# First output projection ahead of the older batch's second one, group norm among the latter's products, first attention begun on half of q and k

## The chip, the cores and the metric

One core of one Trainium2 chip runs the whole program in one launch. The metric is the device time in microseconds; the kernel before takes 4062.5 us (median of 3 runs, 4062.24 to 4063.74). Engines are named as in the profile: PE is TensorE, with its weight loads as PEld, DVE is VectorE, ACT is ScalarE, POOL is GpSimd, and SP is the queue of SyncE, from which nearly all transfers are issued.

## The reference, cut to what matters

Eight batches of 1024 tokens with 512 channels, all float32. Each passes two layers, and each layer is a group norm, an attention and an output projection that is added to the layer's input:

```python
# layer 0: 16 heads of 32 channels
x = x + proj(attention(_gn(x) @ w_qkv, heads=16), w_proj, b_proj)
# layer 1: 4 heads of 128 channels, with position logits
x = x + attention(_gn(x) @ Wq, _gn(x) @ Wk, _gn(x) @ Wv, heads=4, pos_emb_w, pos_emb_h) @ Wo
```

The group norm takes the mean and the variance over all tokens of 16 neighbouring channels, so it cannot begin before the whole x of its batch is there, and no product of the layer can begin before the norm has ended. No batch depends on another.

## The kernel before, in words

Everything is kept transposed, channels on partitions: an activation of one batch is a "block" of 128 x 4 x 1024 floats (2 MB), and eight blocks fit on chip (`BLOCKS`, taken in turn by the tag "block"). What does not fit is put away in DRAM and fetched again (`put_away`, `fetch`, L209 and L216).

**Projections.** Each of the eight weight matrices is applied in seven products instead of eight (a Strassen-like form). `forms` (L319 to L322) makes the sums of the input's quarters on DVE, partly in place. A projection is two units, u = 0 and u = 1, and `seven` makes one unit: seven products into three PSUM banks x, y, z. Between its products stand small operations: y is read by DVE into `a` (L359) after its first product and into `b` (L367) after its second, and only then may the next product accumulate into y. `Plain` puts a result into a block, `Onto` adds it to the fetched x (L418 on POOL, L423 and L425 on DVE). Unit u gives channel chunks u and u + 2. `Stream` holds the order in which weight tiles are loaded (`plan`), one unit ahead; `project_T` and `project_rows` run two units each.

**First attention** (`attention_0`): 64 steps for each batch, over four channel chunks m, two halves h of the queries and eight key blocks j. A step is a score product `ps` (L516, one buffer of four banks), an exponential on ACT (L524), a product with v into `acc` (L535) and a running sum `es` of the exponentials on DVE (L544 for the first two, L546 after that). Eight steps end with the product `sums` (L556), a normalisation on DVE and POOL (L482 to L504), which writes over q.

**Second attention** (`attention_1`): 64 steps of full 128-row products, run as one stretch, with the loading and the norm of the coming batch woven in.

**The order around the change.** The loop over b runs 9 times. Iteration b runs the first attention of batch b (here) beside a list `rest`, in this order: `after_1` of batch b-2 (past: projection WO, result written out), `after_0` of batch b-1 (last: projection WP), `norm_1` of b-1, `second` of b-1 (q, k, v and position logits of the second attention), `attention_1` of b-1 with the load of b+1 (coming), `before_0` of b+1 (q, k, v of the first attention). Parts are Python generators that yield what they cost, two for each product. `side_by_side` emits one step of the attention whenever its share of the total cost is due. `ALONE` is cost that is charged with no product behind it: while norm_1 runs, only attention steps are emitted. A scheduler then orders instructions by readiness, so that the built order differs somewhat from the emitted one. `woven(main, side, start, gap)` puts one piece of a side part behind every gap-th piece of the main part.

**The start.** Batch 0 is loaded and normed, then all six units of q, k and v run with nothing beside them, then iteration 0 runs the first attention of batch 0 beside the load and `before_0` of batch 1.

Of the kernel before, what the change touches and what calls it, by code (L numbers as in the profile page):

```python
# [27 lines left out]
def quick_path(  # L28
# [131 lines left out]
    class Stream:  # L160


        def __init__(self, plan):
            self.plan = [(m, rows, u) for m, rows in plan for u in range(2)]
            self.tiles = {}
            self.at = -1
            for i in ORDER:
                self.load(0, i)
# [77 lines left out]
    def group_norm(st, xT, name):  # L246

        mv = st.pop("mv")

        def averages(out, src, tag):  # L250
            total = small.tile([P, 2], F32, tag=f"total{tag}", name=f"total{tag}_{name}")
            nc.vector.tensor_reduce(
                total, src.rearrange("p (g k) -> p g k", k=GROUP_CHANNELS), axis=AX.X, op=ALU.add
            )
            nc.vector.tensor_scalar(
                out.rearrange("p (g k) -> p g k", k=GROUP_CHANNELS),
                total.unsqueeze(2).to_broadcast([P, 2, GROUP_CHANNELS]),
                1.0 / GROUP_CHANNELS,
                None,
                op0=ALU.mult,  # L260
            )

        turned = small.tile([P, 32], F32, tag="turned", name=f"turned_{name}")
        nc.vector.transpose(turned, mv)
        avg = small.tile([P, 2, 32], F32, tag="avg", name=f"avg_{name}")
        averages(avg[:, 0, :], turned, 0)

        nc.vector.tensor_sub(turned, turned, avg[:, 0, :])
        nc.vector.tensor_mul(turned, turned, turned)
        averages(avg[:, 1, :], turned, 1)  # L270
        back = small.tile([P, 2, 32], F32, tag="back", name=f"back_{name}")
        nc.vector.transpose(back.rearrange("p a c -> p (a c)"), avg.rearrange("p a c -> p (a c)"))
        mean = back[:, 0, :CC]
        var = small.tile([P, CC], F32, tag="var", name=f"var_{name}")
        nc.vector.scalar_tensor_tensor(
            var, back[:, 0, CC : 2 * CC], GN_EPS, back[:, 1, :CC], op0=ALU.add, op1=ALU.add
        )
        rstd = small.tile([P, CC], F32, tag="rstd", name=f"rstd_{name}")
        nc.gpsimd.tensor_tensor(rstd, var, neg_half, op=ALU.pow)
        yield 0  # L280
        for cc in range(CC):
            nc.vector.tensor_scalar(
                xT[cc],
                xT[cc],
                mean[:, cc : cc + 1],
                rstd[:, cc : cc + 1],
                op0=ALU.subtract,
                op1=ALU.mult,
            )
        yield 0  # L290


    in_place = [False]
# [156 lines left out]

        return [[x[n * HC + u][:, h * NB : (h + 1) * NB] for h in range(NH)] for n in range(2)]

    def project_T(fs, m, y, name):

        for u in range(2):
            stream.unit(m, False, u)
            yield from seven(fs, u, False, Plain(halves(y, u)), f"{name}_{u}")

# [46 lines left out]

    def attention_0(q, k, v, b):

        steps = [(m, h, j) for m in range(CC) for h in range(NH) for j in range(NT)]
        state = {}

        def front(m, h, j):
            name = f"0_{b}_{m}_{h}_{j}"
            ps = psum.tile([P, HB, NB], F32, tag="ps", name=f"ps_{name}", bufs=1)
            for r in range(HB):
                rows = slice(r * D0, (r + 1) * D0)
                nc.tensor.matmul(  # L516
                    ps[:, r, :],
                    k[m][rows, j * P : (j + 1) * P],
                    q[m][rows, h * NB : (h + 1) * NB],
                    start=True,  # L520
                    stop=True,
                )
            e = mem.tile([P, HB, NB], F32, tag="e0", name=f"e_{name}", bufs=2)
            nc.scalar.activation(e, ps, AF.Exp, scale=D0 ** -0.5)  # L524
            return e

        def back(m, h, j, e):
            name = f"0_{b}_{m}_{h}_{j}"
            if j == 0:
                state["acc"] = psum.tile([P, NB], F32, tag="acc", name=f"acc_{name}", bufs=1)  # L530
                state["first"] = e
            acc = state["acc"]
            for r in range(HB):
                c0 = (m * HB + r) * D0
                nc.tensor.matmul(  # L535
                    acc[r * D0 : (r + 1) * D0, :],
                    v[:, j, c0 : c0 + D0],
                    e[:, r, :],
                    start=(j == 0),
                    stop=(j == NT - 1),  # L540
                )
            if j == 1:
                state["esum"] = mem.tile([P, HB, NB], F32, tag="es0", name=f"es_{name}", bufs=1)
                nc.vector.tensor_add(state["esum"], state["first"], e)  # L544
            elif j > 1:
                nc.vector.tensor_add(state["esum"], state["esum"], e)  # L546
            if j < NT - 1:
                return
            nc.scalar.copy(q[m][:, h * NB : (h + 1) * NB], acc)
            state["ended"] = (m, h, state["esum"])  # L550

        def finish(m, h, esum):
            name = f"0_{b}_{m}_{h}"
            su = psum.tile([P, NB], F32, tag="acc", name=f"sums_{name}", bufs=1)
            for r in range(HB):
                nc.tensor.matmul(  # L556
                    su[r * D0 : (r + 1) * D0, :],
                    ones[:, :D0],
                    esum[:, r, :],
                    start=True,  # L560
                    stop=True,
                )
            normalise(q[m][:, h * NB : (h + 1) * NB], su, name)

        pending = None
        for at in steps:
            if "ended" in state:
                finish(*state.pop("ended"))
            e = front(*at)
            if pending is not None:  # L570
                back(*pending)
            pending = (*at, e)
            yield 2
        back(*pending)
        yield 1
        finish(*state.pop("ended"))
# [98 lines left out]
    def load(b, st):  # L675
# [19 lines left out]
        st["xn"] = forms(x, f"xn0_{b}")  # L695
        yield 0

    def before_0(b, st, hook=None):

        fs = st.pop("xn")  # L700
# [110 lines left out]
    PRODUCT = 2 * len(ORDER) * HC  # L811
    SECOND = 3 * PRODUCT - 8

    ALONE = 5

    WQ0, WK0, WV0 = [Matrix(w_qkv, i * C, f"qkv{i}") for i in range(3)]
    WP, WQ1, WK1 = Matrix(w_proj, 0, "p"), Matrix(Wq, 0, "q1"), Matrix(Wk, 0, "k1")
    WV1, WO = Matrix(Wv, 0, "v1"), Matrix(Wo, 0, "o")
    FIRST = [(WQ0, False), (WK0, False), (WV0, True)]
    plan = list(FIRST)  # L820
    for b in range(B + 1):
        if b == B:
            plan.append((WP, False))
        if b >= 2:
            plan.append((WO, False))
        if 1 <= b < B:
            plan.append((WP, False))
        if b >= 1:
            plan += [(WQ1, False), (WK1, False), (WV1, True)]
        if b + 1 < B:  # L830
            plan += FIRST
    plan.append((WO, False))

    states = [{} for _ in range(B)]
    WQ0.add_up(nc.vector, nc.scalar, nc.gpsimd, keep=True)
    run(load(0, states[0]))
    for m in (WK0, WV0):
        m.add_up(nc.vector, nc.sync, nc.gpsimd, keep=True)
    stream = Stream(plan)

# [2 lines left out]
            m.add_up(nc.gpsimd, nc.gpsimd, nc.gpsimd)  # L843
            yield 0

    run(before_0(0, states[0]))
    for b in range(B + 1):
        rest, total = [], 0
        s = [None] * 2 + states + [None] * 2
        past, last, here, coming = s[b : b + 4]  # L850
        incoming = load(b + 1, coming) if coming is not None else iter(())

        def forms_0(b=b, st=last):
            st["ao0"] = forms(st["q0"], f"ao0_{b - 1}")

        def forms_past(b=b, st=past):
            forms_1(b - 2, st)

        def forms_last(b=b, st=last):
            forms_1(b - 1, st)  # L860

        if last is not None:
            norm = norm_1(b - 1, last)
            if here is None:
                rest.append(after_0(b - 1, last, forms_past))
                rest.append(woven(later(after_1, b - 2, past), norm, 1, 4))
            else:
                if past is not None:
                    rest.append(after_1(b - 2, past, forms_0))
                    total += PRODUCT  # L870
                rest.append(later(after_0, b - 1, last))
                rest.append(chain([ALONE], (cost + ALONE for cost in norm), marked()))
                total += PRODUCT + 3 * ALONE
            rest.append(later(second, b - 1, last))
            rest.append(woven(later(lambda st: attention_1(*st.pop("at")), last), incoming, 4, 6))
            total += SECOND
        else:
            rest.append(incoming)
        if coming is not None:
            before = later(before_0, b + 1, coming, forms_last if last is not None else None)  # L880
            rest.append(before if last is not None else woven(before, other_sums(), 2, 7))
            total += 3 * PRODUCT
        if here is not None:
            side_by_side(attention_0(here["q"], here["k"], here["v"], b), chain(*rest), total)
        else:
# [494 lines left out]
```

## Time and profile before

| what | value |
|---|---|
| time | 4062.5 us |
| profiled span | 4059.8 us |
| PE busy | 3848.8 us, 95% |
| DVE busy | 2531.9 us, 62% |
| ACT busy | 1719.5 us, 42% |
| POOL busy | 601.6 us, 15% |
| one iteration from b = 2 to b = 6 | about 491 us (the product x_wo begins one at 1341.7 and the next at 1832.6) |
| bytes moved | 234.18 MB, mean 58 GB/s |

The page shows one profiled execution. Its first part gives the busy time of each engine, its second part the span in 40 slices. A busy PE is not PE at its peak, since matmuls are pipelined; what can be won without fewer products is the time in which PE has nothing to do, 211 us here. Answers of the trace name an instruction by engine, line, operation and tiles. In a timeline the columns are start, duration, instruction, count of records, and in brackets the idle time of the engine just before it with what ended that. A product of `seven` is 16 records (x16) or 32 (x32) for v.

### The profile page before, as it was taken

The numbers are of one execution on the slowest core, as the hardware profiler recorded it, in microseconds if no ns is written. First come the engines' busy times: TensorE is split into PE (matmuls) and PEld (weight loads), VectorE is DVE, ScalarE is ACT, GpSimd is POOL, SyncE is SP. The second block draws the span as 40 slices with busy tenths as digits, with TensorE's granted clock in tenths as the row PEclk, the third lists the DMA queues.
The fourth block names the chain that finished last, engine by engine and source line by source line (L and its number), as shares of the span: only waits on it lengthen the run. The fifth ranks groups of instructions, "written<-read, shape, count | busy, mean of one in ns | idle before, by whom it ended". The sixth has DMA issues, their size and how long they took to land.

```text
span 4059.8 us, 71621 instructions
## 1 busy us (share of the span) xinstructions
PE 3848.8 (95%) x30338; PEld 1417.6 (35%) x30338; DVE 2531.9 (62%) x2915; ACT 1719.5 (42%) x1761; POOL 601.6 (15%) x396
## 2 busy tenths in 40 slices
PE   6898899998999989999999999999999998999998
PEld 3232244232443324432244323433234332244353
DVE  5776665576655867458564685646856568664544
ACT  1454443444434444344443444444444444543132
POOL 1331111121111211112110111101111111111101
PEclk9999999999999999999999999999999999999999
DMA  5320120141201512014120231203311031110401
GB/s 143 118 86 26 48 59 6 37 122 50 59 6 38 129 49 58 7 47 131 37 53 12 88 85 36 53 19 95 79 37 45 26 98 54 33 63 8 115 29 22
DMA packets 498694, 234.18 MB, mean 58 GB/s; under 512 B 286368, under 2 KB 478144, under 8 KB 497344
## 3 DMA queue, kind: packets, MB, share of 16 engines
q1 hardware_dynamic: 495232, 214.79, 19.8%
q0 software_dynamic: 2608, 13.70, 0.9%
q8 instruction: 241, 3.95, 0.4%
q10 hardware_dynamic: 528, 1.05, 0.1%
q14 instruction: 85, 0.70, 0.1%
HBM read 170.72 MB, written 58.72 MB: 57 GB/s over the span
## 4 chain that ended last, share of the span: by engine, by line
PE 86%; DVE 7%; ACT 5%; issue 1%; DMA 1%; POOL 0%; SPq 0%; DVEq 0%; ACTq 0%; POOLq 0%
PE ps L516 12%; PE ps L626 11%; PE acc L638 11%; PE acc L535 11%; PE y_q L299 4%; PE y_k L299 3%; PE y_v L299 3%; PE ps L627 3%; ACT e L524 3%; PE x_v L299 3%; PE x_k L299 3%; PE x_q L299 3%; PE z_q L299 3%; PE z_v L299 2%; PE z_k L299 2%; PE y_wp L299 2%
## 5 line engine op out<-in xcount | busy, mean ns | idle before, releaser
L524 ACT ACTIVATE e<-ps 128x2048 f32<-128x2048 f32 x512 | 961.6, 1878 | 873.4 <-PE ps L516 749.1
L546 DVE TENSOR_TENSOR es<-es,e 128x2048 f32<-128x2048 f32 x384 | 899.3, 2342 | 504.5 <-ACT e L524 503.0
L516 PE MATMUL ps<-q,k 32*128 32x512 f32 x4096 | 613.1, 654 | 127.5 <-ACT e L524 127.3
L535 PE MATMUL acc<-e,v 128*32 128x512 f32 x4096 | 557.5, 617 | 12.9 <-ACT su L482 11.9
L629 ACT ACTIVATE e<-ps 128x512 f32<-128x512 f32 x512 | 305.7, 597 | 581.4 <-PE ps L627 551.2
L626 PE MATMUL ps<-q,k 128*128 128x512 f32 x1024 | 523.7, 593 | 0.0
L638 PE MATMUL acc<-e,v 128*128 128x512 f32 x1024 | 521.9, 592 | 0.0
L649 DVE TENSOR_TENSOR es<-es,e 128x512 f32<-128x512 f32 x384 | 287.0, 747 | 267.3 <-ACT e L629 266.5
L627 PE MATMUL ps<-posT,sel 128*128 128x512 f32 x512 | 406.7, 794 | 0.0
L504 POOL TENSOR_TENSOR q<-q,su 128x512 f32<-128x512 f32 x128 | 199.2, 1557 | 1381.7 <-DVE su L500 1339.3
L516 PEld LDWEIGHTS ps<-q,k 32*128 32x128 f32 x4096 | 166.6, 186 | 533.4 <-ACT e L524 267.2
L626 PEld LDWEIGHTS ps<-q,k 128*128 128x128 f32 x1024 | 193.6, 190 | 246.2 <-issue 239.4
L638 PEld LDWEIGHTS acc<-e,v 128*128 128x128 f32 x1024 | 193.1, 189 | 146.7 <-issue 105.2
L535 PEld LDWEIGHTS acc<-e,v 128*32 128x32 f32 x4096 | 82.0, 109 | 409.3 <-issue 352.1
L612 DVE TENSOR_TENSOR posT<-pp,posT 32x512 fp32r<-32x512 f32 x128 | 111.2, 869 | 157.8 <-ACT posT L611 157.3
L544 DVE TENSOR_TENSOR es<-e,e 128x2048 f32<-128x2048 f32 x64 | 173.1, 2704 | 35.7 <-ACT e L524 35.7
L484 DVE STREAM_TRANSPOSE tu<-su 128x512 f32<-128x512 f32 x128 | 90.7, 709 | 116.3 <-ACT su L482 116.0
L611 ACT CAST posT<-pp 32x512 fp32r<-32x512 f32 x128 | 104.8, 819 | 132.2 <-DVE posT L612 87.4
L482 ACT COPY su<-sums 128x512 f32<-128x512 f32 x128 | 74.9, 585 | 160.2 <-PE sums L556 92.1
L408 POOL TENSOR_TENSOR v<-b_v,p_v 128x512 f32<-128x512 f32 x32 | 67.3, 2104 | 499.8 <-ACT p_v L373 479.3
L408 POOL TENSOR_TENSOR k<-b_k,p_k 128x512 f32<-128x512 f32 x32 | 64.0, 1999 | 513.7 <-ACT p_k L373 513.7
L627 PEld LDWEIGHTS ps<-posT,sel 128*128 128x128 f32 x512 | 97.3, 190 | 122.5 <-issue 122.5
(188 smaller groups left out, 4404.1 us busy)
## 6 DMA issues: line engine op xcount, KB each, us to landing
w_qkv<-ws_qkv SPq DMA_DIRECT2D x168, 128.0 KB, 2.5
xs<-in_x SPq DMA_DIRECT2D x256, 64.0 KB, 2.6
d<-x0T SPq DMA_DIRECT2D x32, 512.0 KB, 3.0
x1T<-d SPq DMA_DIRECT2D x32, 512.0 KB, 6.4
d<-x1T SPq DMA_DIRECT2D x32, 512.0 KB, 3.6
x2T<-d SPq DMA_DIRECT2D x32, 512.0 KB, 6.0
out<-ot SPq DMA_DIRECT2D x256, 64.0 KB, 2.0
w_qkv<-in_L_conv_w_qkv SPq DMA_DIRECT2D x126, 128.0 KB, 2.2
```

Of the source, the lines that this page charges most:

```text
L299: ins = nc.tensor.matmul(out[columns, :], weights[:, columns], moving, start=start, stop=stop, skip_group_check=open_sum,)
L504: nc.gpsimd.tensor_tensor(dst, dst, su, op=ALU.mult)
L516: nc.tensor.matmul(ps[:, r, :], k[m][rows, j * P : (j + 1) * P], q[m][rows, h * NB : (h + 1) * NB], start=True, stop=True,)
L524: nc.scalar.activation(e, ps, AF.Exp, scale=D0 ** -0.5)
L535: nc.tensor.matmul(acc[r * D0 : (r + 1) * D0, :], v[:, j, c0 : c0 + D0], e[:, r, :], start=(j == 0), stop=(j == NT - 1),)
L544: nc.vector.tensor_add(state["esum"], state["first"], e)
L546: nc.vector.tensor_add(state["esum"], state["esum"], e)
L626: nc.tensor.matmul(ps, k[h][:, keys], q[:, h, queries], start=True, stop=False)
L627: nc.tensor.matmul(ps, sel[:, keys], posT[:, h, queries], start=False, stop=True)
L629: nc.scalar.activation(e, ps, AF.Exp, scale=1.0 / math.sqrt(D1))
L638: nc.tensor.matmul(acc, v[:, j, h * D1 : (h + 1) * D1], e, start=(j == 0), stop=(j == NT - 1),)
L649: nc.vector.tensor_add(state["esum"], state["esum"], e)
```

## The change

It has three parts.

- **Order.** In iteration b, `after_0` of batch b-1 comes first and `after_1` of batch b-2 second. `norm_1` of b-1 is no longer run alone but woven into the 14 products of `after_1` (start 3, gap 3). Only in iteration 1, where there is no older batch, does it stay alone (`ALONE` is 4 then and is charged four times, since the norm now yields after every second chunk). The weight plan follows.
- **End of an iteration.** Its last seven products (the second unit of v for the coming batch) get no attention steps: their cost of 14 is taken from the total, so the first attention ends before them, and `forms_0`, the sums for the projection WP, is made among them. The sums for WO, which stood there before, are now made in the second unit of `after_0`.
- **Start.** v of batch 0 is projected first, then only u = 0 of q and k, which gives chunks 0 and 2. The first attention takes its chunks in the order 0, 2, 1, 3 and begins at once; u = 1 of q and k runs beside it, woven with the load of batch 1.

```diff
@@ class Stream, group_norm
-            self.plan = [(m, rows, u) for m, rows in plan for u in range(2)]
+            self.plan = plan
...
-        yield 0
+            if cc % 2:
+                yield 0
@@ project_T, attention_0
-    def project_T(fs, m, y, name):
+    def project_T(fs, m, y, name, units=(0, 1)):
...
-        steps = [(m, h, j) for m in range(CC) for h in range(NH) for j in range(NT)]
+        steps = [(m, h, j) for m in (0, 2, 1, 3) for h in range(NH) for j in range(NT)]
@@ new
+    def before_first(st):
+        fs = st["xn"]
+        st["v"] = block("v0_0", [P, NT, C])
+        yield from project_rows(fs, WV0, st["v"], "v0_0")
...
+        yield from project_T(fs, WQ0, st["q"], "q0_0", (0,))
+        yield from project_T(fs, WK0, st["k"], "k0_0", (0,))
+    def rest_of_first(st):
+        fs = st.pop("xn")
+        yield from project_T(fs, WQ0, st["q"], "q0_0", (1,))
+        yield from project_T(fs, WK0, st["k"], "k0_0", (1,))
@@ the loop
-    ALONE = 5
+    ALONE = 4
...
-            if here is None:
-                rest.append(after_0(b - 1, last, forms_past))
-                rest.append(woven(later(after_1, b - 2, past), norm, 1, 4))
+            rest.append(after_0(b - 1, last, forms_past if past is not None else None))
+            total += PRODUCT
+            if past is not None:
+                rest.append(woven(later(after_1, b - 2, past), norm, 3, 3))
+                total += PRODUCT
             else:
-                if past is not None:
-                    rest.append(after_1(b - 2, past, forms_0))
-                    total += PRODUCT
-                rest.append(later(after_0, b - 1, last))
                 rest.append(chain([ALONE], (cost + ALONE for cost in norm), marked()))
-                total += PRODUCT + 3 * ALONE
+                total += 4 * ALONE
             rest.append(later(second, b - 1, last))
+            total += SECOND
+            if here is not None and coming is None:
+                rest.append(at_once(forms_0))
+                total -= 4
...
-            rest.append(incoming)
+            rest.append(woven(rest_of_first(here), incoming, 0, 2))
+            total += PRODUCT
         if coming is not None:
-            before = later(before_0, b + 1, coming, forms_last if last is not None else None)
+            before = later(before_0, b + 1, coming, forms_0 if last is not None else None)
             rest.append(before if last is not None else woven(before, other_sums(), 2, 7))
-            total += 3 * PRODUCT
+            total += 3 * PRODUCT - (PRODUCT // 2 if last is not None else 0)
```

More of the change, by code (lines that the diff above doesn't have):

```diff
@@ L451, in halves @@
         return [[x[n * HC + u][:, h * NB : (h + 1) * NB] for h in range(NH)] for n in range(2)]
-    def project_T(fs, m, y, name):
-        for u in range(2):
+    def project_T(fs, m, y, name, units=(0, 1)):
+        for u in units:
             stream.unit(m, False, u)
@@ L696, in load @@
         yield 0
+    def before_first(st):
+        fs = st["xn"]
+        st["v"] = block("v0_0", [P, NT, C])
+        yield from project_rows(fs, WV0, st["v"], "v0_0")
+        st["q0"] = block("q0_0")
+        st["q"] = chunks(st["q0"])
+        st["k"] = chunks(block("k0_0"))
+        yield from project_T(fs, WQ0, st["q"], "q0_0", (0,))
[4 more added lines that the diff above has]
+        yield from project_T(fs, WK0, st["k"], "k0_0", (1,))
     def before_0(b, st, hook=None):
@@ L818, in quick_path, with units @@
     WV1, WO = Matrix(Wv, 0, "v1"), Matrix(Wo, 0, "o")
-    FIRST = [(WQ0, False), (WK0, False), (WV0, True)]
-    plan = list(FIRST)
+    def units(m, rows=False):
+        return [(m, rows, u) for u in range(2)]
+    FIRST = units(WQ0) + units(WK0) + units(WV0, True)
+    plan = units(WV0, True) + [(m, False, u) for u in range(2) for m in (WQ0, WK0)]
     for b in range(B + 1):
-        if b == B:
-            plan.append((WP, False))
+        if b >= 1:
+            plan += units(WP)
         if b >= 2:
-            plan.append((WO, False))
-        if 1 <= b < B:
-            plan.append((WP, False))
+            plan += units(WO)
         if b >= 1:
-            plan += [(WQ1, False), (WK1, False), (WV1, True)]
+            plan += units(WQ1) + units(WK1) + units(WV1, True)
         if b + 1 < B:
             plan += FIRST
-    plan.append((WO, False))
+    plan += units(WO)
     states = [{} for _ in range(B)]
-    WQ0.add_up(nc.vector, nc.scalar, nc.gpsimd, keep=True)
+    WV0.add_up(nc.vector, nc.scalar, nc.gpsimd, keep=True)
     run(load(0, states[0]))
-    for m in (WK0, WV0):
+    for m in (WQ0, WK0):
         m.add_up(nc.vector, nc.sync, nc.gpsimd, keep=True)
@@ L844, in other_sums, with at_once @@
             yield 0
-    run(before_0(0, states[0]))
+    def at_once(do):
+        do()
+        return
+        yield
+    run(before_first(states[0]))
     for b in range(B + 1):
@@ L851, in quick_path, with forms_0 @@
         incoming = load(b + 1, coming) if coming is not None else iter(())
-        def forms_0(b=b, st=last):
-            st["ao0"] = forms(st["q0"], f"ao0_{b - 1}")
+        def forms_0(b=b, st=here):
+            st["ao0"] = forms(st["q0"], f"ao0_{b}")
         def forms_past(b=b, st=past):
             forms_1(b - 2, st)
-        def forms_last(b=b, st=last):
-            forms_1(b - 1, st)
         if last is not None:
             norm = norm_1(b - 1, last)
-            if here is None:
-                rest.append(after_0(b - 1, last, forms_past))
-                rest.append(woven(later(after_1, b - 2, past), norm, 1, 4))
-            else:
-                if past is not None:
-                    rest.append(after_1(b - 2, past, forms_0))
-                    total += PRODUCT
-                rest.append(later(after_0, b - 1, last))
+            rest.append(after_0(b - 1, last, forms_past if past is not None else None))
[3 more added lines that the diff above has]
+                total += PRODUCT
+            else:
                 rest.append(chain([ALONE], (cost + ALONE for cost in norm), marked()))
-                total += PRODUCT + 3 * ALONE
+                total += 4 * ALONE
             rest.append(later(second, b - 1, last))
+            total += SECOND
+            if here is not None and coming is None:
+                rest.append(at_once(forms_0))
+                total -= 4
             rest.append(woven(later(lambda st: attention_1(*st.pop("at")), last), incoming, 4, 6))
-            total += SECOND
         else:
-            rest.append(incoming)
+            rest.append(woven(rest_of_first(here), incoming, 0, 2))
+            total += PRODUCT
         if coming is not None:
-            before = later(before_0, b + 1, coming, forms_last if last is not None else None)
+            before = later(before_0, b + 1, coming, forms_0 if last is not None else None)
             rest.append(before if last is not None else woven(before, other_sums(), 2, 7))
-            total += 3 * PRODUCT
+            total += 3 * PRODUCT - (PRODUCT // 2 if last is not None else 0)
         if here is not None:
```

## The prediction

> **What bounds the kernel now.** I read the page's engine shares first, then the waits of PE, then the timeline of PE for every gap, and last DVE around the largest gap.
>
> ```profile
> PE 3848.8 (95%) x30338; PEld 1417.6 (35%) x30338; DVE 2531.9 (62%) x2915; ACT 1719.5 (42%) x1761; POOL 601.6 (15%) x396
> ```
> ```profile
> PE ps L516 <- ACT e L524: 127.3, 60, 8.4
> PE x_q L299 <- DVE x0T L282: 35.8, 2, 31.3
> ```
>
> PE sets the pace and no product is removed, so the change can win only idle time (4059.8 - 3848.8 = 211.0 us) and slow matmuls. Of it 127.3 us is `ps` waiting for an exponential: `ps` has one buffer, so a step with no product behind it lasts 3.14 us (1.00 us of wait) while its PE work is 2.08. Two places hold most of it. The first is the norm that runs alone, once in each iteration:
>
> ```profile
> 1430.05 1.14 PE L516 MATMUL ps<-q,k 32*128 32x512 f32 x8 [0.99 <-ACT e L524]
> 1431.12 1.06 PE L535 MATMUL acc<-e,v 128*32 128x512 f32 x8
> 1440.33 2.09 PE L516 MATMUL ps<-q,k 32*128 32x512 f32 x8 [8.14 <-ACT e L524]
> 1442.35 1.94 PE L535 MATMUL acc<-e,v 128*32 128x512 f32 x8
> 1444.06 2.11 PE L299 MATMUL x_q<-x1T,w_q 128*32 128x512 f32 x16
> ```
>
> The reader is to see the 8.14 us gap, and three groups behind it that are longer than elsewhere (1.14, 1.06 and 1.90). With the 1.00 at 1424.88 the loss is 1.00 + 0.99 + 8.14 + 0.95 + 0.88 + 0.21 = 12.2 us. The exponential is late because DVE is: its buffer is freed by an `es` that stands behind the norm and the sums.
>
> ```profile
> 1421.08 2.29 DVE L546 TENSOR_TENSOR es<-es,e 128x2048 f32<-128x2048 f32 x1
> 1423.29 0.74 DVE L425 SCALAR_TENSOR_TENSOR x1T<-z_wp,bproj_sb,x1T 128x512 f32<-128x512 f32 x1
> ...
> 1428.25 2.26 DVE L282 TENSOR_SCALAR x1T<-x1T,back,rstd 128x1024 f32<-128x1024 f32 x3 [1.20 <-POOL rstd L279]
> ...
> 1433.93 2.17 DVE L320 TENSOR_TENSOR f_xn<-f_xn,x1T 128x1024 f32<-128x1024 f32 x1
> 1436.03 2.28 DVE L544 TENSOR_TENSOR es<-e,e 128x2048 f32<-128x2048 f32 x1
> ```
>
> The second place is iteration 0 and its end. Its products run out at about 330 us, and then steps run bare until q is normalised and summed:
>
> ```profile
> 352.65 2.09 PE L516 MATMUL ps<-q,k 32*128 32x512 f32 x8 [2.37 <-ACT e L524]
> ...
> 359.93 1.14 PE L516 MATMUL ps<-q,k 32*128 32x512 f32 x8 [1.00 <-ACT e L524]
> ...
> 375.87 1.87 PE L516 MATMUL ps<-q,k 32*128 32x512 f32 x4 [1.98 <-ACT e L524]
> 379.46 3.63 PE L299 MATMUL y_wp<-f_ao,w_p 128*32 128x512 f32 x16 [1.71 <-DVE f_ao L320]
> ```
>
> **What the Trainium skill says.** "TensorE: Matmul & The Clock Gate", section "What's actually happening": after an idle window of about 3.4 us PE falls to half clock, and about 3.4 us of work brings it back. The trace agrees: 2.09 against 1.14 us behind 8.14 us of idle (even behind 2.37, so the window is not a sharp threshold here). The same page, "Architectural detail": ACT and DVE are strict FIFO. The trace agrees, as above, and this decides the steady part below. "Perfetto Trace Analysis", "Optimization Strategy": regimes with different limits gain from being interleaved. That is the intent here; but the two windows that cover `after_1`, `after_0` and the norm say how little room is left:
>
> ```profile
> 848.00:925.00 77.00, 77.00 (x676) 21.01 (x672) 62.17 (x65) 33.91 (x25) 19.55 (x14) 1.00 0.51 116
> 925.00:955.00 30.00, 21.52 (x132) 4.71 (x128) 24.70 (x34) 11.28 (x9) 3.23 (x3) 0.77 0.17 62
> ```
>
> The columns are PE, PEld, DVE, ACT and POOL busy, clock, DMA share and GB/s. PE is full in the first while DVE fills 81%; put together, DVE brings 86.9 us of work.
>
> **The change part by part.** From PE's timeline a product takes 1.71 us (1352.71 to 1354.42), a step 2.08, both 3.79 (1361.75 to 1365.54), `sums` 0.97.
>
> *Start.* Bare before the first `ps` were 42 products; now 28, so it comes at 108.4 - 14 x 1.71 = 84.4. Iteration 0 then holds 56 products for 64 steps. In the built order the first 42 steps have one each: 42 x 3.79 + 5 x 0.97 = 164.1. Waits there: the trace has 2.45 us (0.69, 0.55, 0.64, 0.57) in the 26 such steps from 131 to 236.7, so 4. The 14 products of v take as long as before, 84 us (236.7 to 322.6, less one wait). The tail to `sums` is 2.5, and 3 I add because the load of batch 1 (about 20 us of DVE: 16 operations of 0.7, the norm, the sums) now stands beside steps that need 2.3 us of DVE in 3.79. So `sums` ends at 338. From there to y_wp the chain is: copy 0.59, tu 0.71, rc and check 0.5, su 0.71, POOL 1.3, f_ao 1.50 and 1.31, gaps 0.6: 7.2, so 345; with 4 for the cold clock and what the same place costs in other waits, 349. Before it was 379.5, with one more product done (1.71). **Gain 29**; bounds 18 (DVE limits the first 14 steps) and 38 (all 33.5 us of waits between 108 and 380 vanish, and 6 of slow matmuls, less 2).
>
> *Iteration 1* keeps the lone norm. Before it lost 9.8 in waits (1.00, 7.62, 0.19, 1.01) and 2 in clock. The built order now has seven bare steps there, so 7 x 1.00 lost, and 7 x 3.14 = 22 us cover the norm's 13. **Gain 5**, bounds 2 and 8.
>
> *Iterations 2 to 6.* The lone norm's 12.2 goes. What replaces it: in the built order DVE does the three x1T, then an `es`, then `a_wo`, and PE's fourth product of `after_1` accumulates into y, which it may only when `a_wo` has read y. Queued behind that product are all of PE, and behind `a_wo` the rest of DVE. Let T be the end of `after_0`'s last product. PE arrives at T + 0.97 + 2 x 2.08 + 3 x 1.71 = T + 10.3. DVE: before, it took z_wp 1.5 us after T. The second unit now also holds the sums for WO (1.50 + 1.31 + 1.21 + 1.37 = 5.4) and 0.6 of a step more (1.2), against 4.1 us of DVE gaps seen from 1401 to 1421; so it is 4.0 late. Then z_wp, statistics and aggregate 1.65, one normalisation 1.94, the small operations 2.0, rstd 1.2: T + 10.8; x1T 2.26, es 2.28, a_wo 0.68: T + 16.0. PE waits 5.7 us. A wait of 4.48 us at 124.57 was followed by groups of 3.64, 1.93 and 2.23 for 1.90, 1.06 and 1.90, so 2.9 more. Loss 8.6, **gain 3.5 each, 17.5 in all**. Bounds: no wait at all (12.2 each) and one as long as before (0). The x1T and x2T transfers now take the blocks of k and v of the ended attention, which are free before the seven bare products: 3.5 MB, about 11 us at the 330 GB/s that the trace reaches, before w_p is needed some 26 us after the last `ps`. Hidden. The seven bare products, 12 us, hide the last normalisation and the sums for WP (9 us): nothing.
>
> *Iteration 7* lost 13.6 in waits and 2.2 in clock. It now has a step per product, where DVE and PE both need about 110 us for 28 products; I put its loss at 11. **Gain 5**, bounds 0 and 13.
>
> *More waits in `second`.* Each of iterations 2 to 6 has one wait of about 2.85 us for an exponential behind the posT casts, iteration 7 has three. Steps per cost go from 65/231 = 0.28 to 65/202 = 0.32, and iteration 7 had 65/147 = 0.44; in proportion 0.5 more waits, 1.4 us, five times: **loss 7**. Bounds 0 and 14. *The end* (iteration 8) keeps its work and had its norm woven already: 0, plus or minus 3.
>
> Sum: 29 + 5 + 17.5 + 5 - 7 = 49.5, so 4062.5 - 49.5 = **4013 us**.
>
> **The rivals.** *The norm is hidden whole.* DVE's lag is absorbed, since it has 38% idle over the span. For it: POOL and DVE did the same weaving in iteration 8, where PE lost only 1.64 + 0.70 + 0.37. Against it: no `es` ran there. 29 + 5 + 5 x 12.2 + 12 - 3 = 104: 3958 us.
>
> *DVE becomes the bound.* Its 86.9 us and the extra steps (2.2 x 2.34) fill the stretch of 87 us entirely, each hiccup is lost, and waits like the old ones come back. Gain of the steady part 0, of iteration 7 0, waits 12: 29 + 5 - 12 = 22: 4040 us.
>
> *The transfers.* If x1T and x2T hold up the weights behind them in the SP queue, by the whole 11 us in each of 6 iterations, with the steady gain 0: 29 + 5 - 7 - 66 = -39: 4102 us. Against it: the free blocks, and DMA at 51% in the busiest window.
>
> **How the numbers follow.** Forecast 0.52, hidden norm 0.19, DVE as bound 0.22, transfers 0.07. Around the forecast its bounds give 3988 to 4036. The range reaches into both faster rivals: 3962 to 4046, leaving out the transfers, part of the hidden norm and the worst of the DVE case. Faster by over 0.2% (below 4054): 0.88; within: 0.05; slower 0.07.
>
> **What would show it.** Right: the first `ps` near 84; y_wp near 349 with no chain of bare steps ahead of it; no gap of 8 us before x_q in iterations 2 to 6, but one of about 6 at y_wo, released by DVE a_wo, with a slow group behind it; the interval between iterations down by 1 to 5 us. Wrong: no such gap (then DVE had room), gaps released by DMA w_p, or DVE busy without a break while PE waits for es.

## The result, and the profile after

The changed kernel takes **4015.99 us** (median, 4013.9 to 4018.04), the kernel before, on the same chip, 4062.37 us (4060.71 to 4063.74). The ratio is 0.9886, with a 95% interval of 0.9869 to 0.9903: 46 us faster. The forecast was 4013.

Line numbers after the change are one or two higher than before, so the norm's `x1T` is L283, `a_wo` L361, `ps` L518 and `acc` L537. First the engine shares of the page, then the waits of PE (in all, times, longest):

```profile
PE 3840.9 (96%) x30338; PEld 1413.9 (35%) x30338; DVE 2527.4 (63%) x2915; ACT 1721.7 (43%) x1761; POOL 604.8 (15%) x396
```
```profile
PE ps L518 <- ACT e L526: 42.3, 33, 7.6
PE y_wo L301 <- DVE a_wo L361: 39.9, 7, 8.0
...
PE sums L558 <- ACT q L551: 16.1, 5, 3.2
```

The same matmuls run, in 8 us less of busy time, and PE's idle time falls from 211.0 to 4015.1 - 3840.9 = 174.2 us. Of the 127.3 us that `ps` waited for exponentials 42.3 are left. But two waits have grown: the one at y_wo from 1.6 to 39.9 us, which the forecast named, and the one at `sums` from 1.5 to 16.1, which it did not. No weight transfer shows among the steady iterations' waits, so the rival with the transfers is out.

PE's timeline of iteration 2 shows the wait that took the place of the lone norm, and DVE's timeline shows what made it:

```profile
869.05 1.90 PE L301 MATMUL x_wo<-q,w_o 128*32 128x512 f32 x16
877.22 3.64 PE L301 MATMUL y_wo<-f_ao,w_o 128*32 128x512 f32 x16 [6.26 <-DVE a_wo L361]
880.79 2.09 PE L518 MATMUL ps<-q,k 32*128 32x512 f32 x8
```
```profile
871.17 3.19 DVE L283 TENSOR_SCALAR x1T<-x1T,back,rstd 128x1024 f32<-128x1024 f32 x3 [1.20 <-POOL rstd L280]
874.28 2.28 DVE L546 TENSOR_TENSOR es<-e,e 128x2048 f32<-128x2048 f32 x1
876.49 0.68 DVE L361 TENSOR_TENSOR a_wo<-y_wo,p_wo 128x512 f32<-128x512 f32 x1
```

PE has ended x_wo at 870.95 and could go on. The product before it on y ended at 867.17, so `a_wo` had its input from then on; it runs at 876.49, behind the norm and an `es`. The group behind the wait is slow (3.64 for 1.90). The same 6.3 us stand in all of iterations 2 to 6.

At the start, y_wp now begins at 353.51 instead of 379.46. In iteration 1 the lone norm still has its gap:

```profile
85.59 1.14 PE L518 MATMUL ps<-q,k 32*128 32x512 f32 x8
...
353.51 3.50 PE L301 MATMUL y_wp<-f_ao,w_p 128*32 128x512 f32 x16 [3.47 <-DVE f_ao L322]
...
407.83 2.09 PE L518 MATMUL ps<-q,k 32*128 32x512 f32 x8 [7.57 <-ACT e L526]
```

Where the time came from, stage by stage. A stage runs from its mark to the next one in PE's timeline of the two profiled executions; the marks are y_wp above, then the first product of iterations 2, 7 and 8. At y_wp the kernel before has one more product behind it, so 1.7 us are moved from the first row to the second.

| stage | before, us | after, us | gain | forecast |
|---|---|---|---|---|
| to y_wp | 379.46 | 353.51 | 24.2 | 29 |
| iteration 1 | 468.66 | 466.53 | 3.8 | 5 |
| iterations 2 to 6 | 2462.50 | 2441.36 | 21.1 | 17.5 - 7 = 10.5 |
| iteration 7 | 431.75 | 435.59 | -3.8 | 5 |
| iteration 8 and the end | 317.43 | 318.11 | -0.7 | 0 |
| sum | 4059.80 | 4015.10 | 44.7 | 49.5 |

### The profile page after: what moved, and what is told of

It reads as the page before. It is cut to its first block, busy times and chain, and to the rows that moved or that the text cites. A ratio compares the mean times of both kernels' runs of the same rounds, so it can differ in the third digit from the quotient of the medians.

```text
span 4015.1 us, 71582 instructions
## 1 busy us (share of the span) xinstructions
PE 3840.9 (96%) x30338; PEld 1413.9 (35%) x30338; DVE 2527.4 (63%) x2915; ACT 1721.7 (43%) x1761; POOL 604.8 (15%) x396
## 4 chain that ended last, share of the span: by engine, by line
PE 85%; DVE 8%; ACT 4%; issue 1%; POOL 1%; DMA 0%; SPq 0%; POOLq 0%; DVEq 0%; ACTq 0%
PE ps L518 12%; PE ps L628 11%; PE acc L640 11%; PE acc L537 11%; PE y_q L301 4%; PE y_v L301 4%; PE ps L629 3%; PE y_k L301 3%; PE x_k L301 3%; PE x_v L301 3%; PE x_q L301 3%; PE z_q L301 3%; PE z_v L301 2%; ACT e L526 2%; PE y_wo L301 2%; PE z_k L301 2%
## 5 line engine op out<-in xcount | busy, mean ns | idle before, releaser
L548 DVE TENSOR_TENSOR es<-es,e 128x2048 f32<-128x2048 f32 x384 | 887.7, 2312 | 459.8 <-ACT e L526 459.0
L518 PE MATMUL ps<-q,k 32*128 32x512 f32 x4096 | 600.1, 652 | 42.4 <-ACT e L526 42.3
L537 PE MATMUL acc<-e,v 128*32 128x512 f32 x4096 | 550.8, 610 | 12.9 <-ACT su L484 10.2
L518 PEld LDWEIGHTS ps<-q,k 32*128 32x128 f32 x4096 | 164.0, 186 | 447.9 <-issue 221.3
L537 PEld LDWEIGHTS acc<-e,v 128*32 128x32 f32 x4096 | 81.7, 108 | 406.1 <-issue 348.5
L301 PE MATMUL y_wo<-f_ao,w_o 128*32 128x512 f32 x768 | 112.2, 654 | 44.1 <-DVE a_wo L361 39.9
L649 DVE TENSOR_TENSOR es<-e,e 128x512 f32<-128x512 f32 x64 | 44.2, 691 | 146.1 <-ACT e L631 146.1
```

What stands on the lines that cost most here:

```text
L301: ins = nc.tensor.matmul(out[columns, :], weights[:, columns], moving, start=start, stop=stop, skip_group_check=open_sum,)
L518: nc.tensor.matmul(ps[:, r, :], k[m][rows, j * P : (j + 1) * P], q[m][rows, h * NB : (h + 1) * NB], start=True, stop=True,)
L537: nc.tensor.matmul(acc[r * D0 : (r + 1) * D0, :], v[:, j, c0 : c0 + D0], e[:, r, :], start=(j == 0), stop=(j == NT - 1),)
```

## The experiments

Two theories stood against each other. **Order:** the new wait comes from `a_wo`'s place in DVE's queue, not from the amount of DVE's work, and another order takes it away. **Load:** DVE is full in this stretch (the rival that called it the bound), and whatever is moved, PE waits elsewhere. All ratios are to the kernel before on the same chip. The changed kernel ran on another chip than the experiments, so a gain over it is taken from the two ratios (0.001 is 4 us), not from the two times.

**1. The start alone.** The loop over b as before; only the start of the change.

```diff
-    run(before_0(0, states[0]))
+    run(before_first(states[0]))
...
-            rest.append(incoming)
+            rest.append(woven(rest_of_first(here), incoming, 0, 2))
+            total += PRODUCT
```

> The kernel before with the change's new start alone (v first, then u = 0 of q and k, chunks 0, 2, 1, 3); its order inside an iteration, the lone norm and the sums for the projections stay as before. If the two parts of the change are independent, as the forecast adds them: in the changed kernel y_wp starts 26.0 us earlier than before, less 1.7 for one product that is still to come, so 4062.4 - 24 = 4038, with y_wp near 355 and the gaps of 7 to 8 us before x_q still in iterations 1 to 6. If the start only pays together with the new order (the rival that hides the norm gives the order nearly all of the gain): above 4050.

Measured: 4036.04 us, ratio 0.9940 (0.9926 to 0.9953). y_wp starts at 351.3, the first `ps` at 84.38, and the gaps of 7.5 to 8.2 us are there in iterations 1 to 7 (one in each).

**2. The order alone.** The changed kernel with the old start.

```diff
-    run(before_first(states[0]))
+    run(before_0(0, states[0]))
...
-            rest.append(woven(rest_of_first(here), incoming, 0, 2))
-            total += PRODUCT
+            rest.append(incoming)
```

> The changed kernel with the start of the kernel before (all six units of q, k and v first). Forecast: what is left is the order, 2 in iteration 1, 4.2 in each of iterations 2 to 6, -3.8 in iteration 7: 4016 + 24 = 4040, and the waits of y_wo for a_wo stay at 6.3 and 8.0 us. If the parts depend on one another, the two gains (this one and the start's) do not add up to 46.

Measured: 4037.63 us, ratio 0.9946 (0.9932 to 0.9960); y_wo waits 6.25 us in iterations 2 to 6 and 7.98 in iteration 7. The two losses of ratio, 0.0060 and 0.0054, add to 0.0114, which is that of the whole change: within their intervals the parts add up, and each brings about half.

**3. The normalisations held back.** An instruction can be tied behind the one that was emitted before it on its engine. Here that is done to the four x1T normalisations; DVE does the same work in another order.

```diff
-            nc.vector.tensor_scalar(
+            ins = nc.vector.tensor_scalar(
                 xT[cc],
...
+            tc.keep_in_program_order(ins) if "1_1" <= name <= "1_6" else None
```

> The changed kernel; the four normalisations of x1T (batches 1 to 6) are held behind the DVE work that was emitted before them, so that a_wo no longer stands behind three of them. Same work on every engine, another order on DVE. Forecast's cause (order in DVE's queue): the statistics and the first es (2.3 us) still stand ahead of a_wo, so the wait of y_wo falls from 6.3 to about 2 and the cold group behind it may go: 5 to 6 us in each of six iterations, 4016 - 33 = 3983. Rival (DVE is the bound, its work fills the stretch): the wait goes elsewhere, into ps waiting for e, and the time stays within 5 us of 4016.

Measured: 3982.86 us, ratio 0.9805 (0.9791 to 0.9818). Its PE timeline at the same place:

```profile
867.80 1.90 PE L301 MATMUL x_wo<-q,w_o 128*32 128x512 f32 x16
871.58 1.92 PE L301 MATMUL y_wo<-f_ao,w_o 128*32 128x512 f32 x16 [1.88 <-DVE a_wo L361]
```

The wait is 1.88 us, and the group behind it is not slow (1.92). By the ratios 33 us are gained over the changed kernel.

**4. The whole norm held back.** The same for the first operation of the statistics alone, so that `a_wo` and `b_wo` of the first unit come before the norm begins.

```diff
-        nc.vector.transpose(turned, mv)
+        ins = nc.vector.transpose(turned, mv)
+        tc.keep_in_program_order(ins) if "1_1" <= name <= "1_6" else None
```

> The changed kernel; the first operation of the norm's statistics (the transpose of mv, batches 1 to 6) is held behind the DVE work emitted before it, so that a_wo and b_wo of the first unit come ahead of the whole norm. Same work, another order. Forecast's cause: a_wo ends by 869.7 in iteration 2, before PE asks for it at 871.0; the wait of y_wo vanishes, and the norm, now some 10 us later, still ends before x_q, which comes 39 us behind that wait: up to 6.3 + 2.7 (cold groups) in five iterations and 8 + 3 in iteration 7, less a wait of some 3 us where the next es stands behind the norm: 4016 - 40 = 3976. Rival (DVE is the bound): within 5 us of 4016.

Measured: 3974.43 us, ratio 0.9788 (0.9775 to 0.9801). DVE's and PE's timelines:

```profile
868.89 2.25 DVE L546 TENSOR_TENSOR es<-e,e 128x2048 f32<-128x2048 f32 x1
871.06 0.68 DVE L361 TENSOR_TENSOR a_wo<-y_wo,p_wo 128x512 f32<-128x512 f32 x1
```
```profile
870.67 1.90 PE L301 MATMUL x_wo<-q,w_o 128*32 128x512 f32 x16
872.38 1.90 PE L301 MATMUL y_wo<-f_ao,w_o 128*32 128x512 f32 x16
```

`a_wo` ends at 871.74, before PE asks for it, and y_wo follows without a wait. Some of it comes back later: 0.77 us at a `ps` and 1.37 us at the second unit's y_wo in each iteration. The load theory allowed 5 us of change; by the ratios 33 us (experiment 3) and 40 us (here) came from order alone. Order is shown.

**5. No bare tail.** Steps beside all products again, the sums for WP at the start of `after_0`.

```diff
-            before = later(before_0, b + 1, coming, forms_0 if last is not None else None)
+            before = later(before_0, b + 1, coming, None)
...
-            total += 3 * PRODUCT - (PRODUCT // 2 if last is not None else 0)
+            total += 3 * PRODUCT
```

> The changed kernel without its step-free end of an iteration: steps run beside all 28 + 42 products again, and the sums for WP are made at the start of after_0 instead of among the last seven products. Forecast (the seven bare products hide the last normalisation and the sums for WP, some 9 us): without them PE meets the same wait as at the end of iteration 0, 3.5 us at y_wp released by DVE f_ao plus 1.6 of cold group, in six iterations 31, less about 3 for steps that stand further apart: 4016 + 28 = 4044. Rival (bare products bring nothing, they only crowd the steps elsewhere): 4016 or below, with fewer waits of ps in second.

Measured: 4041.74 us, ratio 0.9954 (0.9938 to 0.9971). A line of PE's waits:

```profile
PE y_wp L301 <- DVE f_ao L322: 31.2, 7, 4.6
```

Six waits of 4.63 us come to the one of 3.46, and slow groups behind most of them. The bare products do hide the sums for WP, and by the ratios they are worth some 28 us to the changed kernel. The rival was right in part: with the steps further apart, PE's waits at `sums` fall from 16.1 to 3.2 us and at `acc` (behind `su`) from 10.2 to 3.4. So the bare products do crowd the steps elsewhere, at a smaller price than what they hide.

**6. More work ahead of `a_wo`.**

```diff
                 statistics(st, xT, n * HC + u, f"1_{b}")
+                again = [nc.vector.bn_stats(...) for h in range(NH) if u]
```

> The changed kernel with four more bn_stats of x1T in the second unit of after_0 (their output is not used), 4 x 0.65 = 2.6 us of DVE work that stands ahead of the norm and so ahead of a_wo. Forecast's cause (a_wo's place in DVE's queue; the norm starts when after_0's last operations have passed DVE): the wait of y_wo grows from 6.3 to 8.9 in iterations 2 to 6 and from 8.0 to 10.6 in iteration 7, and iteration 1's lone gap grows alike: 4016 + 7 x 2.6 = 4034. Rival (DVE has slack in that stretch that takes it up): below 4022.

Measured: 4019.03 us, ratio 0.9897 (0.9881 to 0.9914), far from the expected 4034. The wait of y_wo grew only from 6.26 to 6.53. DVE's timeline says why:

```profile
873.14 2.25 DVE L546 TENSOR_TENSOR es<-e,e 128x2048 f32<-128x2048 f32 x1
...
876.66 0.81 DVE L283 TENSOR_SCALAR x1T<-x1T,back,rstd 128x1024 f32<-128x1024 f32 x1 [1.20 <-POOL rstd L280]
877.39 0.68 DVE L361 TENSOR_TENSOR a_wo<-y_wo,p_wo 128x512 f32<-128x512 f32 x1
```

The scheduler answered with another order: `es` ahead of the norm's last small operation, and one normalisation instead of three ahead of `a_wo`. So the run changed two things at once and does not measure what a microsecond of DVE work costs there; that stays open.

**7. The casts first.** The waits in `second` lie behind the position products (`pp`). There each cast on ACT waited for the subtraction on DVE before it, as ACT's timeline of the changed kernel shows at the new wait of `sums`:

```profile
1043.65 0.58 ACT L613 CAST posT<-pp 32x512 fp32r<-32x512 f32 x1 [1.10 <-DVE posT L614]
1044.26 1.88 ACT L526 ACTIVATE e<-ps 128x2048 f32<-128x2048 f32 x1
1046.03 0.58 ACT L551 COPY q<-acc 128x512 f32<-128x512 f32 x1
```
```profile
1046.66 1.94 PE L558 MATMUL sums<-es,ones 128*32 128x512 f32 x8 [3.23 <-ACT q L551]
```

What makes a cast wait for the subtraction before it, which writes other elements of the tile, no run shows. The experiment emits the four casts before the four subtractions.

```diff
-            for r in range(2):
-                for u, view in enumerate((by_y, by_x)):
+            for do in range(2):
+              for r in range(2):
+                for u, view in enumerate((by_y, by_x)):
...
-                    nc.scalar.copy(view[rows], pp[rows])
-                    nc.vector.tensor_sub(view[rests], pp[rows], view[rows].bitcast(F32))
+                    nc.scalar.copy(view[rows], pp[rows]) if do == 0 else nc.vector.tensor_sub(view[rests], pp[rows], view[rows].bitcast(F32))
```

> The changed kernel; for each of the four position products the four casts on ACT are emitted first and the four subtractions on DVE after them, in place of cast, subtraction, cast, subtraction. Same work. If the waits in second (1.2 for e, 1.7 for su, 3.2 for the copy of acc with 1.6 of cold groups) come from ACT and DVE waiting for one another by turns (6.4 us from the first cast to the next e at 969.1, where the casts take 3.3), e comes 2.5 us earlier and most of these waits go: 7 in each of iterations 2 to 6, 10 in iteration 7: 4016 - 45 = 3971. Rival (the waits come from the number of steps per product, as the forecast's term for second had it): within 10 us of 4016, the waits as before.

Measured: 3961.38 us, ratio 0.9754 (0.9737 to 0.9770). ACT's timeline (the cast is one line further down there), and two lines of PE's waits:

```profile
963.01 3.34 ACT L614 CAST posT<-pp 32x512 fp32r<-32x512 f32 x4 [1.36 <-PE pp L601]
```
```profile
PE sums L558 <- ACT q L551: 1.4, 5, 0.3
...
PE acc L537 <- ACT su L484: 0.4, 1, 0.4
```

The casts run back to back in 3.34 us; the next `e` begins 4.5 us after the first of them (967.52), where it took 6.4, and the waits of `sums` and `acc` go from 16.1 and 10.2 us to 1.4 and 0.4. The gain of 54 us is more than the 45 expected. The waits in `second` need this alternation. The number of steps, the rival cause, has a part in them too: from the first x_q of iterations 2 to 6 to their ends PE waits 30.7 us in the changed kernel, 16.6 in experiment 5, which has fewer steps to a product, and 1.4 here. So how many steps run there decides how much of the alternation PE meets.

**8. Both.** The orders of 4 and 7 together.

> Both at once: the norm's statistics held behind a_wo and b_wo, and the casts first. If the two places are independent: 3974 - 45 = 3930. If DVE is the bound once its waits are gone: above 3955.

Measured: **3919.97 us**, ratio 0.9660 (0.9644 to 0.9676), 140 us below the kernel before on the same chip and, by the ratios, 92 below the changed kernel. The two gains, 40 and 54, add up: DVE is still not the bound.

**9. Iteration 1.** Kernel 8, with iteration 1's normalisations tied behind the `es` emitted ahead of them.

```diff
+            tc.keep_in_program_order(ins) if name == "1_0" else None
```

> stats_casts, and in iteration 1 the normalisations of x1T are held behind the es that were emitted before them, so that the first es no longer waits behind three of them. Same work. This tests the step of the prediction that failed in iteration 1 (seven bare steps at 1.00 each and no gap of 8 us). If the gap of 7.6 us comes from the place of the first es in DVE's queue, it goes, the bare steps run at 3.14 us each, and x_q begins some 6 us earlier: 3920 - 6 = 3914. Rival (the gap is the norm's own length, which x_q must wait for in any case): the wait moves to x_q or y_q, and the time stays at 3920.

Measured: 3918.93 us, ratio 0.9650 (0.9637 to 0.9663); the interval does not tell it from kernel 8. The timelines do. The first `es` now comes right behind the statistics, and the gap is 4.15 us instead of 7.57:

```profile
399.74 2.28 DVE L546 TENSOR_TENSOR es<-e,e 128x2048 f32<-128x2048 f32 x1
```
```profile
404.04 1.65 PE L518 MATMUL ps<-q,k 32*128 32x512 f32 x8 [4.15 <-ACT e L526]
```

x_q begins at 419.19, in kernel 8 at 423.02: 3.8 us of the 6 expected, since `es` still waits for the statistics, which fill DVE until 399.7.

## Why the prediction was right, and where not

**Total.** 4013 against 4016, but the terms did not all hold: iterations 2 to 6 gave 10.6 more than forecast, the start 5 less, iteration 7 nine less. That these nearly cancel, and the total is only 3 us off, is luck.

**Start (29 forecast, 24.2 in the trace, 24 by experiment 1's ratio).** The first `ps` is right (84.4 forecast, 84.38 with the start alone, 85.59 in the changed kernel). The waits between it and `sums` are right too: 4, 2.9 (the 84 us of v hold the old waits of 1.41 and 1.48) and 3 were allowed for, 9.9, and the ten gaps in the timeline add up to 10.4. Two slips of the working cancel. 84.4 + 164.1 + 4 + 84 + 2.5 + 3 is 342, and the prediction says 338. And the 4 us for the cold clock do not move y_wp's start at all, because the old start was followed by an equally slow group (3.63 before, 3.50 now). Without either slip y_wp still comes out at 349; it begins at 353.5. Of these 4 us, 1.2 is the later first `ps`, 0.5 the waits, and 0.4 the chain from `sums` to y_wp (7.6 us, from 345.9, for 7.2). The other 2.3 is work between the first `ps` and `sums` that lasts longer than allowed for; why stays open, and the profiled runs with this start put y_wp anywhere from 351.32 to 355.35.

**Iteration 1 (5 forecast, 3.8).** The step is wrong, and that the size is near is luck. "Seven bare steps, so 7 x 1.00 lost" overlooked that the third bare step's exponential needs a buffer which only the first `es` frees, and that stood behind three normalisations as before: 7.57 us. So PE's waits up to the first x_q grew, from 9.8 to 11.8 us, where 7 were forecast. The stage gained all the same because the waits behind x_q fell, from 8.1 to 4.7 us, and slow groups there went (a y_k of 3.18 for 1.90 before), which the forecast had not priced. Experiment 9 moves that `es` ahead and shortens the gap, so its place is part of the cause; by the timeline the statistics ahead of it are the rest, but no run takes them away.

**Iterations 2 to 6, the norm (3.5 each forecast, about 4.5 measured).** The first x_q parts the norm from `second`. In the five iterations it begins 102.4 us behind the first product before and 95.7 to 96.1 after, with one step of 2.1 us less ahead of it: 32.7 - 10.4 = 22.3 us in all, for 17.5. The mechanism is right and shown: the lone norm's gap is gone, y_wo waits for `a_wo` because of DVE's order, 6.26 us for 5.7 forecast. PE's arrival was T + 10.3, as forecast (T is 860.63). DVE is 0.5 later than T + 16.0, and the three x1T alone take 3.19 instead of 2.26. Experiments 3 and 4 leave 1.88 and 0 us of the wait, with the same work. Two sizes were off. The 12.2 us of the old loss were read from iteration 3; its waits of 10.1 us were only 8.5 and 8.4 in iterations 2 and 6. And one thing had no price: before, the score product just ahead of the old gap ran in two pieces, each of which lasts about as long as a whole one (1.14), and now it runs whole, about 1 us in each iteration:

```profile
1424.88 1.12 PE L516 MATMUL ps<-q,k 32*128 32x512 f32 x2 [1.00 <-ACT e L524]
...
1426.93 1.13 PE L516 MATMUL ps<-q,k 32*128 32x512 f32 x6
```

The experiments also answer the two rivals: the norm could be hidden nearly whole, though not by this change (experiment 4 leaves 2.1 us of waits ahead of x_q in an iteration, of 9.5 before), and DVE was not the bound.

**"More waits in second" (-7 forecast, about -1 measured).** What lies behind x_q became 11.6 us longer in the five iterations, and the step that moved there is 10.4 of it. The number that fails is 0.5 more waits of 2.85 us for each iteration. The one wait of 2.85 shrank to 1.20, one of 1.04 vanished, and one of 3.23 us came at `sums`: in five iterations 28.1 us of waits before and 30.7 after, 2.6 more. What was not priced is the slow group. Before, two nearly equal gaps differ in what stands behind them:

```profile
1010.90 2.04 PE L516 MATMUL ps<-q,k 32*128 32x512 f32 x8 [2.88 <-ACT e L524]
1503.45 1.14 PE L516 MATMUL ps<-q,k 32*128 32x512 f32 x8 [2.85 <-ACT e L524]
```

The gap left PE slow in iterations 2, 4 and 5 (2.88, 2.91 and 2.86 us; the `ps` behind it 2.04 to 2.09) and not in 3 and 6 (2.85 and 2.83; 1.14). Those three iterations last 493.0 to 494.4 us, the other two 490.7 and 490.9. After the change all five last 488.1 to 488.8, each with a slow `sums` behind its 3.23 us (1.94 for 1.06). In all, the waits of PE in these iterations fell by 13.5 us (75.5 to 62.0) and its busy time by 7.6: 6.2 of that ahead of x_q, when the moved step is set aside, and 1.4 behind it.

**Iteration 7 (5 forecast, -3.8).** Waits fell there by 2.2 us (26.1 to 23.9): in the part ahead of `second` by about 4, much as forecast, and in `second` they grew by about 2. PE's busy time grew by 6.1; slow groups stand behind the 8 us at y_wo (the next `ps` 1.91 for 1.14) and behind the waits in `second` (at 3464 a `ps` of 2.09, an `acc` of 1.94 and a y_k of 3.06 for 1.14, 1.06 and 1.90). The forecast priced more waits in `second` for iterations 2 to 6 only, and for iteration 7 it named neither more waits there nor slow groups behind the new wait.

**Hidden work.** The seven bare products "hide the last normalisation and the sums: nothing" is right for the sums, as experiment 5 shows; the last normalisation was not tried alone. The transfers are hidden: no wait for w_p appears in any run.

## What to carry to other kernels

When work moves in beside products, look at what already waits in the same queue: a long operation that is ready first can stand ahead of a short one that the bound engine needs, and a scheduler by readiness can put it there, as this one did. Tie the long operation behind the short one before concluding that the engine is full; here that was worth 40 us, nearly as much as the change itself (46). Where two engines share a small job, try giving each its pieces in a row, not by turns; here that was worth 54 us.

## What the runs showed of the hardware that I had not expected

**Slow groups behind short gaps.** The Trainium skill, "TensorE: Matmul & The Clock Gate", section "What's actually happening", gives about 3.4 us of idle window for the half clock, free-running. The runs agree for the long gaps (3.64 us for 1.90 behind 6.26 us, in each of iterations 2 to 6). Shorter ones go both ways. There were slow groups behind 2.86 us and even behind 1.71, where another gap of 1.98 stood shortly ahead (the y_wp at 379.46 of the kernel before, 3.63 us); and behind 3.84 us, at the x_q that waits for its weights in iteration 8 of experiment 8's run, there was none (1.92), nor behind 1.88 in experiment 3. A forecast has to price a gap of 2 to 4 us as one that may or may not cost up to 3 us more: behind the 2.91 us of iteration 4 in the kernel before, `ps`, `acc` and y_k took 2.09, 1.94 and 3.10 for 1.14, 1.06 and 1.90.

**POOL and DVE block one another.** The skill's "SBUF — State Buffer", section "🔬 SBUF: two separate sides", describes an exclusive lock on ports that DVE and POOL share. The traces agree: POOL's product q with su took 1.27 us from 867.51 in the changed kernel and 3.18 us from 869.11 in experiment 4, where DVE's `es` had begun at 868.89 and ran for 2.25 us: POOL ended 1.15 us behind it. The norm's small subtraction (128x32) lasts 0.19 us at the median and 1.15 (from 867.68) beside that product of POOL's. The three x1T of 3.19 us for 2.26 ran beside POOL's x2T (871.11 to 872.37), which would account for the half microsecond by which the forecast missed `a_wo`; no run isolates it.
